# A graph network on one core: 36 sorted blocks instead of 32, 21 gathered instead of 20, and the gather lists made ahead of the first panel

## The chip, the cores and the metric

The kernel runs on one core of one Trainium2 chip. The metric is the device time of one execution in microseconds (us). The engines are named as in the profile: PE (matmuls; PEld its weight loads), DVE (vector), ACT (scalar), POOL (GpSimd, which here mostly issues DMAs with an index for each row), SP (issues plain DMAs).

## What is computed

6250 nodes with 256 features, 100000 random edges, sorted by destination. Cut to what matters:

```python
def agg(h):
    return jax.ops.segment_sum(h[src], dst, num_segments=N)
for l in range(NL - 1):                       # three layers, 256 wide
    h = x + agg(x)
    h = relu(h @ W1s[l] + b1s[l])
    h = relu(h @ W2s[l] + b2s[l])
    x = h @ W3s[l] + b3s[l]
h = x + agg(x)                                # the last layer, 64 wide inside
h = relu(h @ cW1 + cb1)
h = relu(h @ cW2 + cb2)
return h @ cW3 + cb3
# ahead of it: h = max(layernorm(x), 0) goes in; behind it: x + result
```

All of it is float32. The graph is drawn at run time, so the kernel has to look at the edges itself.

## The kernel before

The nodes stand in 49 tiles of 128 (`NT`). Since a sum over edges and a product commute, the table from which each layer reads holds z = h @ W1 already (W3 of a layer is multiplied into W1 of the next), and a layer is: sum z over the edges, add the own row and the bias, relu, two products, store the next z.

**Two ways to sum over the edges.** A block is 128 destination nodes.

- *Multiplied* blocks: an adjacency matrix (counts, one byte each) of 6250 sources by 128 destinations is built in layer 0 and kept in DRAM (`mat`). A *panel* is 3 or 4 such blocks side by side, 384 or 512 columns. `product(l, p)` (L2060 on) walks over the 49 source tiles in the order `ORDER`; for each, ACT casts the bytes to float (`a`, L2052), and PE does four matmuls (agg, L2087: two column halves, and z split into a high and a low part in `XY`). Behind a panel come its relu (L2098) and the MLP (`ps`, L1567 and L1666, with `zz` on DVE, L1671), spread between the matmuls of the next panel.
- *Gathered* blocks: for these POOL fetches, for each k, the k-th neighbour's row of all 128 nodes at once, with one indirect DMA (L1761). DVE adds the rows up two at a time (`sums`, L1798), adds the own row (`u`, L1812 and L1816), PE transposes the block (`pt`, L1825), and it joins the MLP. A block costs as many gathers as its largest degree.

To make gathering cheap the nodes of 32 blocks (`NS`) are *ranked by degree* ("s" blocks; block 0 has the smallest degrees); the other 17 blocks ("u") stay as they are. Of the s blocks the 20 lowest are gathered in layers 0 to 2 (284 rows of each node in all, and in layer 0 one more for each block, the own row), 19 in the last layer (267). The other 29 (30 in the last) are multiplied. Layers 0 to 2 take eight panels, the last layer too.

**Results.** z of u blocks goes back to its place in `XY` and to the table directly. s blocks hold nodes from anywhere, so POOL *scatters* them, one indirect DMA for each block (`place_rows`, L600, with a one-word memset as a mark between two, L598). Once all are placed, `pairs_back` reads the s tiles back two at a time (`turned`, three in flight) and splits them into `XY` (ACT L1391, DVE L1392). `ORDER` walks over the u tiles first, to give this time. The first gather of the next layer waits for all writes to the table. In the last layer s blocks are added into the output, in the same way.

**The rush.** The last gathered block of layers 0 to 2 is a single one. It has its own short MLP (`rush`, L1498, L1514, L1527), since the scatter behind it opens the next layer.

**What sets the order.** The program is written out whole by a planner in Python. It keeps a clock of the PE work it has emitted (`passed`), and class `ByNode` spreads the gathers over a layer: `begin` sets the first date (the clock plus a lag of 9 or 12 us) and a pace from the layer's PE work, less `close`; `ready` says when the sums of a pair of rows are emitted on DVE; `send` emits the gathers, each tied behind the last paced PE instruction (`after`), so POOL cannot run ahead of PE by more than the plan. Constants: `AHEAD_OF` (how much ahead of the layer's end the gathering shall be done), `SLOW` (us planned for a unit ahead of the first panel). Every engine works strictly in its written order.

**Layer 0.** Ahead of the panels, input rows are normalized, and the edges are looked up and the nodes ranked (until about 125 us). Then `build` makes the adjacency in *units*: DVE compares (hi and lo one-hots, L1234), PE multiplies them (bp, L1288), ACT casts (`at`, L1296), SP stores. `PRE` = 28 units come ahead of the first panel, the others between the matmuls of the panels. The *lists* (`listed`, L1848 on) say which node stands at each rank and where its edges are. For every four s blocks DVE makes three tiles (`lane`, `block` and `moved`, L1854 to L1863), PE sums them (L1870), then POOL fetches the edge lists (L1886), and DVE makes row indices of them (`idxN`). Four values, as bf16 digits in `V` = 6 columns, are carried to the ranks: the node (two digits), its degree, and the start of its edges (three digits). In before all this stands in the first panel, a step at every other source tile; later it makes the codes of the s blocks that are multiplied (12 of them, with one that is built in any case).

Of the kernel before, what the change touches and what calls it, by code (L numbers as in the profile page):

```python
# [9 lines left out]
F32 = mybir.dt.float32  # L10
# [9 lines left out]
P = 128  # L20
# [400 lines left out]
def sorted_edges(  # L421
# [69 lines left out]
    NS = 32  # L491
# [3 lines left out]
    seq = [("u", b) for b in range(NS, NT - 3)] + [("s", b) for b in range(NS - 1, NS - 13, -1)] + [  # L495
        ("u", b) for b in range(NT - 3, NT)] + [("s", NS - 13)]
    early = [(0, 3)] + [(b, 4) for b in range(3, 23, 4)] + [(23, 3), (26, 3)]
    wide = [(b, 4) for b in range(0, 20, 4)] + [(20, 3), (23, 3), (26, 3)]
# [3 lines left out]
    nodes_of = [[(16, 4), (12, 4), (8, 4), (4, 4), (1, 3), (0, 1)]] * NLAYER + [  # L502
        [(15, 4), (11, 4), (7, 4), (3, 4), (1, 2), (0, 1)]]
# [35 lines left out]
    V = 6  # L539
    what = const.tile([P, NS, V], BF16, name="what")  # L540
# [354 lines left out]
    def ranking(pool):  # L895
# [5 lines left out]
        nc.gpsimd.tensor_copy(what[:, :, 0], place[:, 0:1].to_broadcast([P, NS]))  # L901
        nc.gpsimd.tensor_copy(what[:, :, 1], colf[:, :NS])
# [46 lines left out]
        nc.scalar.copy(what[:, :, 2], ps[:, :NS])  # L949
# [14 lines left out]
        at = pool.tile([P, NS], I32, name="at_i", bufs=1)  # L964
        nc.vector.tensor_tensor(at, ps[:, :NS], begins, OP.add)
# [36 lines left out]
        bits = pool.tile([P, 3, NS], I32, name="bits", bufs=1)  # L1002
        nc.vector.tensor_scalar(bits[:, 0], at, P - 1, None, op0=OP.bitwise_and)
        nc.vector.tensor_scalar(bits[:, 1], at, 7, None, op0=OP.arith_shift_right)
        nc.vector.tensor_scalar(bits[:, 2], at, 14, None, op0=OP.arith_shift_right)
        nc.vector.tensor_scalar(bits[:, 1], bits[:, 1], P - 1, None, op0=OP.bitwise_and)
        nc.vector.tensor_copy(what[:, :, 3:], bits.rearrange("p v g -> p g v"))
# [119 lines left out]
    with tc.manual_schedule():  # L1127
# [261 lines left out]
        def split(j, m, z):  # L1389

            nc.scalar.copy(XY[:, j:j + m, :C], z[:, :m, :])  # L1391
            later(1, lambda: nc.vector.tensor_tensor(XY[:, j:j + m, C:], z[:, :m, :],  # L1392
                                                     XY[:, j:j + m, :C].bitcast(F32), OP.subtract))
# [7 lines left out]
        def bring():  # L1401
            while wanted and lent[0] < BACK:
# [11 lines left out]
                def back(j=j, z=z):  # L1414
                    split(j, 1, z)
                    later(1, given)
# [7 lines left out]
        def pairs_back(l):  # L1424
# [6 lines left out]
            def more_pairs(wait):  # L1431
                while left and out[0] < PAIRS:
# [6 lines left out]
                    def back(j=j, z=z):  # L1439
                        split(j, 2, z)  # L1440
                        later(1, done)
# [7 lines left out]
            more_pairs(6)  # L1449
# [12 lines left out]
        def store(l, runs, m):  # L1462

            key = f"table{l + 1}"
            for rows, k, kind, b in runs:
# [17 lines left out]
                if kind == "u" and all((l, j) in used for j in fresh):  # L1483
                    split(b, k, rows)
# [223 lines left out]
        class ByNode:  # L1708
# [110 lines left out]
            def finish(self, b, n, g, u):  # L1819
                def turn():  # L1820
# [15 lines left out]
                    if g == n - 1:  # L1836
                        mlp(self.l, [("s", b + q) for q in range(n)], h1, b == 0 or closing, far)

                closing = self.l < NLAYER and b == self.blocks[-2][0]
                far = FAR - 2 if b == self.blocks[-2][0] else FAR  # L1840
                if b == 0 and self.l < NLAYER:
                    halves(2, lambda: rush(self.l, b, u))
                elif b == 0 or closing and g == n - 1:
                    later(2 if b == 0 else 1, turn)
# [4 lines left out]
        def listed(pool, ps_b):  # L1849

            pieces, G4 = [], 4
            for g0 in range(0, NS, G4):
                lane = pool.tile([P, G4, P], BF16, name="lane", bufs=2)
# [8 lines left out]
                moved = pool.tile(shape, BF16, name="moved", bufs=2)  # L1862
# [13 lines left out]
            begin = pool.tile([P, NS], F32, name="begin")  # L1876
            nc.vector.scalar_tensor_tensor(begin, got[:, 4], float(P), got[:, 3], op0=OP.mult,
# [20 lines left out]
            for _ in range(7):  # L1898
                yield
# [322 lines left out]
```

## Time and profile before

| | |
|---|---|
| runs (us) | 1987.24, 1989.18, 1993.07; median 1989.18 |
| the profiled execution (us) | 1992.96, span 1991.1 |
| mean granted clock of PE | 0.966 |
| instructions in the span | 29317 |
| first agg matmul | 153.31 us |
| layer 0 ends (last panel's relu) | 672.88 us |
| layer 1, layer 2 end | 1112.49, 1550.53 us |

The span is what the trace covers; 1.9 us of the execution lie around it. Lines such as L2087 are lines of the kernel. In a group "x66 | 62.7, 949 | 20.1 <-PE agg L2087 10.1" means 66 instructions, 62.7 us busy, 949 ns each, 20.1 us of idle time in front of them, of which 10.1 ended with that release. In a window's row the columns are the stretch, its length, then busy us of PE, PEld, DVE, ACT and POOL with instruction counts, the granted clock of PE as a share, the share of the DMA engines and GB/s. In the timeline the columns are start, duration, engine, line and operation, and in brackets the idle time in front and what ended it.

### The profile page before, as it was taken

The numbers are of one execution on the slowest core, as the hardware profiler recorded it, in microseconds if no ns is written. First come the engines' busy times: TensorE is split into PE (matmuls) and PEld (weight loads), VectorE is DVE, ScalarE is ACT, GpSimd is POOL, SyncE is SP. The second block draws the span as 40 slices with busy tenths as digits, with TensorE's granted clock in tenths as the row PEclk, the third lists the DMA queues.
The fourth block names the chain that finished last, engine by engine and source line by source line (L and its number), as shares of the span: only waits on it lengthen the run. The fifth ranks groups of instructions, "written<-read, shape, count | busy, mean of one in ns | idle before, by whom it ended". The sixth has DMA issues, their size and how long they took to land. (4 is left out here: it accounts for less than half of the span.)

```text
span 1991.1 us, 29317 instructions
## 1 busy us (share of the span) xinstructions
PE 1853.7 (93%) x9334; PEld 1483.0 (74%) x9334; DVE 915.1 (46%) x1915; ACT 1210.6 (61%) x2370; POOL 1338.7 (67%) x1496
## 2 busy tenths in 40 slices
PE   4868999999999899999999899999999899999896
PEld 3746666776788777777898777777898777777774
DVE  6789788676564243332333343333334353332232
ACT  3766666676666476566566376565665576665562
POOL 2521777777777566676777566677777567777775
PEclk9878999999999999999999899999999999999898
DMA  5523665666556485565566575555566676665663
GB/s 176 176 97 115 182 195 168 203 215 217 168 174 211 157 281 181 154 199 172 178 189 212 166 232 164 163 174 165 165 195 197 193 223 208 173 180 149 147 181 81
DMA packets 247119, 357.22 MB, mean 179 GB/s; under 512 B 33368, under 2 KB 201880, under 8 KB 246666
## 3 DMA queue, kind: packets, MB, share of 16 engines
q0 software_dynamic: 65584, 167.88, 29.2%
q1 hardware_dynamic: 179184, 184.72, 28.6%
q10 hardware_dynamic: 2186, 2.65, 0.4%
q8 instruction: 75, 1.23, 0.2%
q14 instruction: 90, 0.74, 0.1%
HBM read 289.20 MB, written 70.92 MB: 181 GB/s over the span
## 5 line engine op out<-in xcount | busy, mean ns | idle before, releaser
L2087 PE MATMUL agg<-a,XY 128*128 128x512 f32 (+1 forms) x6272 | 1471.4, 387 | 14.5 <-ACT a L2052 11.0
L1761 POOL DMA_INDIRECT rows<-table,idxN x1119 | 1076.6, 962 | 422.0 <-PE agg L2087 207.1
L2087 PEld LDWEIGHTS agg<-a,XY 128*128 128x128 f32 x6272 | 1150.1, 191 | 212.5 <-ACT a L2052 21.2
L2052 ACT CAST a<-at 128x512 fp32r<-128x512 uint8 (+1 forms) x1561 | 876.7, 585 | 328.6 <-PE agg L2087 317.9
L1798 DVE TENSOR_TENSOR sums<-sums,rows 128x512 f32<-128x512 f32 x471 | 328.5, 697 | 650.2 <-DMA rows<-table,idxN 627.0
L1296 ACT CAST at<-bp 128x392 uint16<-128x392 f32 x213 | 102.8, 488 | 119.9 <-PE bp L1288 115.8
L1567 PE MATMUL ps<-h,w 128*128 128x512 f32 (+1 forms) x312 | 132.5, 568 | 4.1 <-DVE zz L1671 3.1
L600 POOL DMA_INDIRECT table<-zz,ids x96 | 96.5, 1005 | 55.8 <-DVE zz L1533 23.0
L1666 PE MATMUL ps<-w,h 128*128 128x256 f32 x576 | 133.2, 384 | 0.0
L1666 PEld LDWEIGHTS ps<-w,h 128*128 128x128 f32 x576 | 110.8, 194 | 15.1
L1288 PE MATMUL bp<-hi,lo 128*128 128x98 bf16 x964 | 88.6, 219 | 32.5 <-DVE lo L1234 25.2
L1288 PEld LDWEIGHTS <-lo 128*128 128x128 bf16 x964 | 54.3, 103 | 86.1 <-DVE lo L1234 42.4
L1234 DVE TENSOR_TENSOR lo<-lanes,pairs 128x512 bf16<-128x512 bf16 x240 | 99.3, 423 | 31.4 <-PE bp L1288 30.1
L1567 PEld LDWEIGHTS ps<-h,w 128*128 128x128 f32 x312 | 60.0, 194 | 56.7 <-issue 38.4
L1671 DVE TENSOR_TENSOR zz<-ps,w 128x512 f32<-128x512 f32 x78 | 49.6, 647 | 103.2 <-PE ps L1666 102.1
L1570 ACT ACTIVATE h<-ps,bias 128x512 f32<-128x512 f32 (+1 forms) x78 | 49.8, 656 | 55.8 <-PE ps L1567 55.8
L1833 ACT ACTIVATE h<-pt,bias 128x256 f32<-128x256 f32 (+1 forms) x80 | 32.7, 460 | 83.3 <-PE pt L1825 83.3
L1234 DVE TENSOR_TENSOR hi<-hi,pairs 128x784 bf16<-128x784 bf16 x120 | 69.3, 578 | 4.2
L1234 DVE TENSOR_TENSOR hi<-cols,pairs 128x784 bf16<-128x784 bf16 x120 | 67.2, 560 | 0.6 <-ACT pairs L1222 0.6
L1886 POOL DMA_INDIRECT lane<-padded,at x20 | 20.3, 1016 | 65.5 <-PE bp L1288 59.7
L1392 DVE TENSOR_TENSOR XY<-turned,XY 128x512 fp32r<-128x512 f32 x48 | 32.7, 694 | 67.4 <-ACT XY L1391 67.3
L600 POOL DMA_INDIRECT out_dram<-zz,ids x32 | 50.8, 1588 | 15.2 <-issue 7.1
(261 smaller groups left out, 958.5 us busy)
## 6 DMA issues: line engine op xcount, KB each, us to landing
at<-mat SPq DMA_DIRECT2D x112, 448.0 KB
mat<-at SPq DMA_DIRECT2D x30, 784.0 KB
at<-mat SPq DMA_DIRECT2D x62, 336.0 KB
rows<-table,idxN POOLq DMA_INDIRECT x1119
turned<-table SPq DMA_DIRECT2D x48, 256.0 KB
at<-mat SPq DMA_DIRECT2D x50, 224.0 KB
at<-mat SPq DMA_DIRECT2D x84, 112.0 KB
own<-zz SPq DMA_DIRECT2D x59, 128.0 KB
```

Of the source, the lines that this page charges most:

```text
L600: got = nc.gpsimd.indirect_dma_start(out=ap, out_offset=bass.IndirectOffsetOnAxis(ap=ids[:, b:b + 1], axis=0), in_=sb, in_offset=None, **kw)
L1234: nc.vector.tensor_tensor(o, values, which[:, :, None, :].to_broadcast(shape), op)
L1288: mm = nc.tensor.matmul(bp[:, m * HW:(m + 1) * HW], lo[:, m, :], hi[:, m, :], start=(i == 0), stop=(i == len(sets) - 1))
L1296: nc.scalar.copy(o, v)
L1567: mm = nc.tensor.matmul(ps[:, :w], weights[l][0][:, c, i * P:(i + 1) * P], h1[:, c, :w], start=(c == 0), stop=(c == KC - 1))
L1570: later(soon, lambda: nc.scalar.activation(h2[0][:, i, :w], ps[:, :w], AF.Relu, bias=b2[l][:, i:i + 1]))
L1666: mm = nc.tensor.matmul(o, h2[0][:, c, nodes], w3[:, c, :], start=(c == 0), stop=(c == KC - 1))
L1671: later(soon, lambda: nc.vector.tensor_tensor(z[:, :m, :], v, w3[:, KC:, :].to_broadcast([P, m, C]), OP.add))
L1761: got = nc.gpsimd.indirect_dma_start(out=t[:, c % 2, :], out_offset=None, in_=tables[self.l][:, :], in_offset=bass.IndirectOffsetOnAxis(ap ...
L1798: nc.vector.tensor_tensor(sums, sums, rows.rearrange("p h c -> p (h c)"), OP.add)
L2052: nc.scalar.copy(o, v)
L2087: mm = nc.tensor.matmul(agg[c][:, :w], XY[:, j, o:o + P], a[:, :w], start=(i == 0 and half == 0), stop=(i == NT - 1 and half == 1))
```

## The change

- `NS` goes from 32 to 36; 13 blocks stay unsorted. Layers 0 to 2 gather 21 blocks (291 rows for each node, in layer 0 with own rows 312), the last layer 19 (257 rows). 28 blocks are multiplied in layers 0 to 2: in layer 0 four panels of 3 and four of 4, in layers 1 and 2 seven panels of 4. The last layer keeps its 30 in eight panels. There are 36 scatters a layer and 18 pairs to read back.
- The block that is gathered last, alone, is the one with most rows (block 20 with 17; in the last layer block 18 with 16) and no longer block 0 with 10.
- The lists are made in the stretch ahead of the first panel, one step at each of the 28 units, with three float32 values (node, degree, start of edges) and no digits; the tiles for them are borrowed from the gathers' pool (`rows`). The edge lists of the first two groups of blocks are fetched there, the others in the first panels, between the codes of the s blocks that are multiplied (one step at every third source tile). Gathering in layer 0 begins as soon as the first list is there.
- Planner: `AHEAD_OF` 4 to 8, `SLOW` 1.0 to 1.8; two pairs fewer of delay in front of the first read-back (6 to 4); at the end of every layer all sums are emitted, in before only in the last; the last layer's copies of x into the output (`own_rows`) are spaced otherwise. `renewed` is a check of the program's order and emits nothing.

The diff's core:

```diff
-    NS = 32
+    NS = 36
-    early = [(0, 3)] + [(b, 4) for b in range(3, 23, 4)] + [(23, 3), (26, 3)]
-    wide = [(b, 4) for b in range(0, 20, 4)] + [(20, 3), (23, 3), (26, 3)]
+    early = [(b, 3) for b in range(0, 12, 3)] + [(b, 4) for b in range(12, 28, 4)]
+    wide = [(b, 4) for b in range(0, 28, 4)]
-    nodes_of = [[(16, 4), (12, 4), (8, 4), (4, 4), (1, 3), (0, 1)]] * NLAYER + [
-        [(15, 4), (11, 4), (7, 4), (3, 4), (1, 2), (0, 1)]]
+    nodes_of = [[(16, 4), (12, 4), (8, 4), (4, 4), (0, 4), (20, 1)]] * NLAYER + [
+        [(14, 4), (10, 4), (6, 4), (2, 4), (0, 2), (18, 1)]]
...
-    V = 6
-    what = const.tile([P, NS, V], BF16, name="what")
+    V = 3
+    what = const.tile([P, NS, V], F32, name="what")
...
-            more_pairs(6)
+            more_pairs(4)
...
-                if self.l == NLAYER and now[0] >= ends[self.l] - 2:
+                if now[0] >= ends[self.l] - (2 if self.l == NLAYER else 0):
                     return True
...
+                final = b == self.blocks[-1][0]
                 closing = self.l < NLAYER and b == self.blocks[-2][0]
-                if b == 0 and self.l < NLAYER:
+                if final and self.l < NLAYER:
                     halves(2, lambda: rush(self.l, b, u))
...
+            def wide_tile(n, m):
+                t = gath.tile([P, 2, C], F32, name="rows").rearrange("p h c -> p (h c)")
+                return t[:, :G4 * n * m].rearrange("p (g v b) -> p g v b", g=G4, v=n)
             for g0 in range(0, NS, G4):
-                lane = pool.tile([P, G4, P], BF16, name="lane", bufs=2)
+                lane = wide_tile(1, P)[:, :, 0]
...
-                moved = pool.tile(shape, BF16, name="moved", bufs=2)
+                moved = wide_tile(V, NS)
...
-            for b0, n in lists_of:
-                for b in range(b0, b0 + n):
-                    fetch(run[:, starts_of[b]:starts_of[b] + wide_of[b]], wide_of[b], b)
-            yield
+            fetch_list(0)
+            yield
+            fetch_list(1)
...
+            for _ in range(3):
+                yield
+            make_list(0)
+            for _ in range(4):
+                yield
+            make_list(1)
...
-        LAGS, CLOSE, AHEAD_OF, NEAREST, CLOSING = (9.0, 12.0), 2.0, 4.0, 5.0, 40.0
+        LAGS, CLOSE, AHEAD_OF, NEAREST, CLOSING = (9.0, 12.0), 2.0, 8.0, 5.0, 40.0
-        COLS, FULL32, TURN, BUILD, SLOW, BURST = 0.457e-3, 1.68e-3, 0.4, 0.25, 1.0, 0.3
+        COLS, FULL32, TURN, BUILD, SLOW, BURST = 0.457e-3, 1.68e-3, 0.4, 0.25, 1.8, 0.3
...
-                if beside is not None and (p or i % 2):
+                if beside is not None and i % 3 == 0:
                     next(lists, None)
...
                 tick(layers[0])
                 layers[0].advance()
+                next(lists)
```

More of the change, by code (lines that the diff above doesn't have):

```diff
@@ L963, in ranking @@
         nc.tensor.matmul(ps[:, :NS], one_b, small, start=False, stop=True)
[L964 to L965 removed]
+        nc.vector.tensor_tensor(what[:, :, 2], ps[:, :NS], begins, OP.add)
         yield
@@ L1950, in listed @@
                     yield
+                if j % 3 == 0:
+                    fetch_list(2 + j // 3)
+                    if j and 1 + j // 3 < len(lists):
+                        make_list(1 + j // 3)
                 if j < HELD:
```

87 lines of the change are left out of this document (44 added, 43 removed).

## The prediction

> **What bounds the kernel now.** I read first the busy shares of the page and its two costliest groups: the line of all engines, then the matmuls that sum over sources (agg) and the row gathers.
>
> ```profile
> PE 1853.7 (93%) x9334; PEld 1483.0 (74%) x9334; DVE 915.1 (46%) x1915; ACT 1210.6 (61%) x2370; POOL 1338.7 (67%) x1496
> L2087 PE MATMUL agg<-a,XY 128*128 128x512 f32 (+1 forms) x6272 | 1471.4, 387 | 14.5 <-ACT a L2052 11.0
> L1761 POOL DMA_INDIRECT rows<-table,idxN x1119 | 1076.6, 962 | 422.0 <-PE agg L2087 207.1
> ```
>
> PE looks like the only bound. An average over stages can hide others, so next came the windows by stage: PE, PEld, DVE, ACT, POOL busy, then the granted clock.
>
> ```profile
> 124.00:153.00 29.00, 12.29 (x112) 8.31 (x112) 27.89 (x66) 14.81 (x40) 3.68 (x3) 0.53 0.35 127
> 153.00:212.00 59.00, 51.84 (x384) 43.20 (x384) 55.15 (x132) 39.48 (x97) 19.12 (x19) 0.94 0.40 122
> 212.00:673.00 461.00, 441.44 (x2609) 332.50 (x2608) 303.94 (x738) 298.94 (x626) 344.00 (x366) 0.98 0.61 192
> 673.00:1112.00 439.00, 427.39 (x1915) 351.65 (x1914) 149.12 (x249) 267.38 (x495) 304.38 (x338) 0.99 0.60 191
> 1112.00:1550.00 438.00, 428.44 (x1918) 353.85 (x1917) 149.69 (x248) 263.71 (x489) 303.36 (x340) 0.98 0.59 181
> ```
>
> The stretch in front of the first panel (124 to 153) belongs to DVE: 27.89 of 29 us. In the first panel (153 to 212) DVE and PE are both nearly full. In the rest of layer 0 and in layers 1 and 2 PE sets the pace, with POOL at about 70%. Two narrower views of POOL, 1403 to 1500 and then 1133 to 1230, say what that 70% means.
>
> ```profile
> L1761 POOL DMA_INDIRECT rows<-table,idxN x66 | 62.7, 949 | 20.1 <-PE agg L2087 10.1 <-issue 5.8 <-PE ps L1567 0.9
> L600 POOL DMA_INDIRECT table<-zz,ids x11 | 10.9, 990 | 2.6 <-issue 2.1 <-DVE sums L1794 0.3 <-DVE sums L1798 0.2
> L598 POOL MEMSET mark<- 1x4 f32 x8 | 0.7, 91 | 0.0
> L1761 POOL DMA_INDIRECT rows<-table,idxN x66 | 62.8, 951 | 36.3 <-PE agg L2087 27.3 <-DVE sums L1798 2.6 <-issue 2.1
> ```
>
> Late in a layer, busy and idle time make up the whole window: 62.7 + 20.1 + 10.9 + 2.6 + 0.7 = 97.0 of 97 us. There the engine is full: a gather costs (62.7 + 20.1)/66 = 1.254 us, a scatter with its mark (10.9 + 2.6 + 0.7)/11 = 1.29. Early in a layer a gather takes 1.50 us, because rows are released only as PE advances. The last view is the timeline at the ends of layers 0 to 2, where the last gathered block is rushed through PE (pt), and its scatter opens the next layer's gathers.
>
> ```profile
> 672.88 1.05 ACT L2098 ACTIVATE h<-agg,bias 128x384 f32<-128x384 f32 x2 [4.74 <-PE agg L2087]
> 680.75 0.44 PE L1498 MATMUL pt<-ident,u 128*128 128x128 f32 x2 [3.45 <-DVE u L1816]
> 1112.49 1.05 ACT L2098 ACTIVATE h<-agg,bias 128x384 f32<-128x384 f32 x2 [0.39 <-PE agg L2087]
> 1119.71 0.69 PE L1498 MATMUL pt<-ident,u 128*128 128x128 f32 x2 [2.79 <-DVE u L1812]
> 1229.46 1.27 ACT L2098 ACTIVATE h<-agg,bias 128x512 f32<-128x512 f32 x2 [0.73 <-PE agg L2087]
> 1550.53 1.05 ACT L2098 ACTIVATE h<-agg,bias 128x384 f32<-128x384 f32 x2 [0.39 <-PE agg L2087]
> 1551.93 0.95 POOL L1761 DMA_INDIRECT rows<-table,idxN  x1 [0.30 <-issue]
> 1557.88 0.44 PE L1498 MATMUL pt<-ident,u 128*128 128x128 f32 x2 [2.93 <-DVE u L1812]
> ```
>
> The ACTIVATE rows mark panel ends. PE already waits about 3 us per layer for the rushed block, so POOL is nearly as long as PE. From rush to rush a middle layer takes 1119.71 − 680.75 = 438.96 and 1557.88 − 1119.71 = 438.17 us. I make the sum between these points.
>
> **The change, part by part.** Where numbers are of the changed program's order, they are counts of instructions.
>
> *Lists in front of the first panel.* On DVE, in that stretch, before: compares alone (hi, lo) that build the adjacency.
>
> ```order
> L1234 TENSOR_TENSOR hi<-cols,pairs 128x784
> L1234 TENSOR_TENSOR hi<-hi,pairs 128x784
> L1234 TENSOR_TENSOR lo<-lanes,pairs 128x512
> L1303 TENSOR_TENSOR at<-at,ident 128x128
> L1234 TENSOR_TENSOR lo<-lanes,pairs 128x512
> ```
>
> And after (the tiles called rows hold lane and moved, the one-hots that sort the nodes):
>
> ```order
> L1227 TENSOR_TENSOR hi<-cols,pairs 128x784
> L1227 TENSOR_TENSOR hi<-hi,pairs 128x784
> L1859 TENSOR_TENSOR rows<-lanes,goal 128x512
> L1863 TENSOR_TENSOR block<-lanes,goal 128x144
> L1868 TENSOR_TENSOR rows<-block,what 128x432
> L1227 TENSOR_TENSOR lo<-lanes,pairs 128x512 x2
> ```
>
> Nine such groups of three moved onto the full engine. Their prices are in the first panel's groups of before (DVE, then PE; the page's row of sums stands last):
>
> ```profile
> L1234 DVE TENSOR_TENSOR lo<-lanes,pairs 128x512 bf16<-128x512 bf16 x40 | 16.1, 418 | 1.4 <-PE bp L1288 1.4
> L1234 DVE TENSOR_TENSOR hi<-hi,pairs 128x784 bf16<-128x784 bf16 x20 | 11.3, 567 | 0.7
> L1234 DVE TENSOR_TENSOR hi<-cols,pairs 128x784 bf16<-128x784 bf16 x20 | 11.2, 558 | 0.0
> L1863 DVE TENSOR_TENSOR moved<-block,what 128x768 bf16<-128x768 bf16 x8 | 7.7, 958 | 0.3
> L1854 DVE TENSOR_TENSOR lane<-lanes,goal 128x512 bf16<-128x512 bf16 x8 | 5.5, 683 | 0.0
> L1858 DVE TENSOR_TENSOR block<-lanes,goal 128x128 bf16<-128x128 bf16 x8 | 2.3, 282 | 0.0
> L1880 DVE SCALAR_TENSOR_TENSOR at<-got,begin 128x32 int32<-128x32 f32 x1 | 0.2, 192 | 0.0
> L1870 PE MATMUL sums<-moved,lane 128*128 128x192 bf16 x32 | 4.4, 263 | 1.0 <-DVE moved L1863 1.0
> L1288 PE MATMUL bp<-hi,lo 128*128 128x98 bf16 x156 | 14.3, 215 | 5.9 <-DVE lo L1234 5.9
> L1798 DVE TENSOR_TENSOR sums<-sums,rows 128x512 f32<-128x512 f32 x471 | 328.5, 697 | 650.2 <-DMA rows<-table,idxN 627.0
> L1886 POOL DMA_INDIRECT lane<-padded,at x20 | 20.3, 1016 | 65.5 <-PE bp L1288 59.7
> ```
>
> A group costs 0.683 + 0.29 + 0.958 × 432/768 = 1.51 us; nine cost 13.6. About 24 short operations (copies, list indices, limits) at some 0.2 each add 5, and three sums at 0.697 add 2: 21 us. DVE is in order and must also wait for what it asked for: a list reads four fetches, 4 × (1.016 + 0.30) = 5.3 us and a landing, with some 3 us of compares between; the first sums wait for rows behind eleven fetches. I take 6, bounded by 0 and 13. So **+27** (21 to 34). Nothing hides it; PE has 12.29 us of work there.
>
> [...]
>
> *The first panel.* It loses list work (7.7 + 5.5 + 2.3 on DVE, 4.4 on PE) and 11 of 39 build units (44 of 156 bp matmuls): on DVE 11 × (16.1 + 11.3 + 11.2)/39 = 10.9. DVE falls from 55.15 to about 44, with 13 sums and the code of two blocks added; PE to 51.84 − 4.4 − 44 × 0.092 = 43. I take 50 us for 59, **−9** (bounds −14 and 0), since waits for rows remain.
>
> *The rest of layer 0.* One block fewer is multiplied. The price of width comes from two views of PE, 1230 to 1343 and 1452 to 1492; the next two rows are of 212 to 673.
>
> ```profile
> L2087 PE MATMUL agg<-a,XY 128*128 128x512 f32 x393 | 95.4, 400 | 0.0
> L2087 PE MATMUL agg<-a,XY 128*128 128x384 f32 x197 | 36.2, 342 | 0.0
> L1288 PE MATMUL bp<-hi,lo 128*128 128x98 bf16 x696 | 62.0, 211 | 10.4 <-DVE lo L1234 7.6 <-ACT at L1296 2.6
> L1825 PE MATMUL pt<-ident,u 128*128 128x128 f32 x38 | 7.5, 281 | 3.3 <-DVE u L1816 3.3
> ```
>
> 95.4/393 = 0.243 and 36.2/197 = 0.184 us, so a block is 196 × 0.059 = 11.5 us. The 11 units come back here: 44 × 62.0/696 = 3.9. The first gather of before, on POOL's timeline, is
>
> ```profile
> 213.81 0.94 POOL L1761 DMA_INDIRECT rows<-table,idxN  x1 [0.30 <-issue]
> ```
>
> Rows are now gathered from the stretch on, so the 3.3 us wait of pt should go. **−11** (−7 to −14). Layer 0 ends 27 − 9 − 11 = 7 us later.
>
> *The rush.* PE at the end of layer 1, before:
>
> ```order
> L1567 MATMUL ps<-h_11943,w_8247 128x384 x4
> L2087 MATMUL agg<-a,XY 128x512 x4
> L1498 MATMUL pt<-ident,u 128x128 x2
> L2087 MATMUL agg<-a,XY 128x512 x4
> L1514 MATMUL ps<-h1s,w_8247 128x128 x4
> ```
>
> And after:
>
> ```order
> L2106 MATMUL agg<-a,XY 128x512 x16
> L1497 MATMUL pt<-ident,u 128x128 x2
> L2106 MATMUL agg<-a,XY 128x512 x4
> L1513 MATMUL ps<-h1s,w_8319 128x128 x4
> L1566 MATMUL ps<-h_11701,w_8319 128x512 x4
> ```
>
> Before, pt stands four matmuls into the next layer, behind the last panel's first product; now four matmuls ahead of the end, in the panel's own last source tile: about 1.7 us before the end, if the rows are there. In layer 0 POOL has room (344 of 461 us), so I take that: 672.88 + 7 − 1.7 = 678.2 against 680.75, **−2.6**.
>
> *Layers 1 and 2.* Gathers go from 284 to 291 and scatters from 32 to 36; PE loses 11.5 us in each. After the second panel the program still has 220 gathers and 30 scatters ahead of the last row: 220 × 1.254 + 30 × 1.29 = 314.6 us. The five panels beside them hold 5 × 196 × 0.243 = 238 us of agg and, by PE's groups of layer 1 below (673 to 1112), 5/7 of 44.8 + 44.3 for the MLP: 302 us.
>
> ```profile
> L1567 PE MATMUL ps<-h,w 128*128 128x512 f32 (+1 forms) x104 | 44.8, 575 | 2.4 <-DVE zz L1671 2.1 <-ACT h L2098 0.3
> L1666 PE MATMUL ps<-w,h 128*128 128x256 f32 x192 | 44.3, 383 | 0.0
> ```
>
> So POOL takes over. From rush to rush: 1.7, two panels at 115 (before 1229.46 − 1112.49 = 117.0, of which some 3 was the rush wait), 314.6, and 6 from the last row to pt (1557.88 − 1551.93): 437.3. That is **−1.7** and **−0.9** (±5 each). The 11.5 us of PE turn into waits at pt. AHEAD_OF and SLOW only move the planner's dates; they change none of these counts.
>
> *The last layer.* Its blocks are multiplied as before. The rush stands before the end rather than 7 us behind it, so the first two panels lie wholly behind it: +3. Gathers fall by 10 (−12.5), four scatters to the output are added, by the row below at (50.8 + 15.2)/32 = 2.06 and a mark, +8; most of it in the covered first panels. I take **+2** (−4 to +6).
>
> ```profile
> L600 POOL DMA_INDIRECT out_dram<-zz,ids x32 | 50.8, 1588 | 15.2 <-issue 7.1 <-DVE zz L1650 7.0 <-DVE sums L1798 0.6
> ```
>
> The sum: −2.6 − 1.7 − 0.9 + 2 = −3.2. The profiled execution took 1992.96 us (span 1991.1 and 1.9 around it), 3.8 over the median 1989.18. So 1989.8 profiled, and a median of **1986.0**.
>
> **The rivals.** *A, PE keeps the bound.* If POOL gets rows earlier than my count releases them (the idle 36.3 us early in a layer being used), each middle layer ends with PE: up to 11 us less each, 1964 in full, about 1975 with half. For it: that idle time is there. Against: its releaser is PE's own progress, and the count has it in.
>
> *B, DVE waits in order at the start: slower.* POOL must send 28 fetches and 42 rows by the end of the first panel: 70 × 1.27 = 89 us from about 158 (two thirds through the stretch, when the lists' sums are done), thus to 247, while the panel would end near 230. The sums stand between the compares on DVE, and PE's builds wait for those. It decides if the sums' rows come later than their place, at about 180 and 230: 4 us more in the stretch and 10 in the panel, 1986 + 14 = 2000. For it: the sums' 627.0 us of idle time ended by gathers. Against: that idle time harmed nothing while DVE had slack.
>
> [...]
>
> That the change fails to do what it says is excluded: the order shows lists, widths and rush moved.
>
> **How the numbers follow.** Forecast 0.53, A 0.21, B 0.21, C 0.05. The terms' bounds, taken together, give 1975 to 1997 for the forecast alone; half of A and B reach to 1971 and 2001, my range. A measurement can tell 0.3%, 6 us: 1983.2 to 1995.1 is "same". Faster: A's 0.20 and 0.15 of the forecast, 0.35. Slower: B's 0.18 and 0.03 of the forecast, 0.21. The rest is 0.44.
>
> **What would show it.** First agg near 180; layer 0's end near 680; POOL's busy and idle time filling whole windows from the third panel on in layers 1 and 2; PE waiting at pt for u by some 8 us or more; 437 from rush to rush. If PE has no wait there and the layers take 426, A holds; a first panel ending near 245, B. Wrong would be above all a first agg before 170, or middle layers that differ by over 6 us from 437.

## The result, and the profile after

The changed kernel took 2003.89 us (median of five runs, 2000.80 to 2007.42) against 1989.18: a ratio of 1.0075, with a 95% interval of [1.0054, 1.0096]. That is slower by less than 1%, but clear of the noise. The forecast was 1986.0 and the range ended at 2001. The profiled execution took 2000.80 us, the lowest of the five, and that of before 1992.96, near the top of its own. So the two traces account for 7.8 of the 14.7 us between the medians; what lies between executions of one kernel, no trace shows.

The page's first line and two of its groups, the gathers and the transpositions of gathered blocks, and behind them the transpositions of before:

```profile
PE 1821.2 (91%) x9056; PEld 1421.7 (71%) x9056; DVE 921.2 (46%) x1928; ACT 1173.1 (59%) x2256; POOL 1375.6 (69%) x1547
L1760 POOL DMA_INDIRECT rows<-table,idxN x1130 | 1087.1, 962 | 417.6 <-PE agg L2106 182.4
L1824 PE MATMUL pt<-ident,u 128*128 128x128 f32 x158 | 32.1, 286 | 47.6 <-DVE u L1811 46.5
```
```profile
L1825 PE MATMUL pt<-ident,u 128*128 128x128 f32 x152 | 30.4, 283 | 20.5 <-DVE u L1812 17.2 <-DVE u L1816 3.3
```

PE has 32.5 us less to do and the kernel is longer all the same: 46.5 us of PE's idle time now end with u, the sum of a gathered block (20.5 before). The windows by stage (the stretch ahead of the first panel, the first panel, the rest of layer 0, layers 1 and 2):

```profile
122.00:176.00 54.00, 25.03 (x188) 20.54 (x188) 47.27 (x124) 18.14 (x46) 22.67 (x22) 0.64 0.29 93
176.00:237.00 61.00, 50.78 (x374) 43.76 (x374) 41.57 (x122) 33.30 (x79) 45.78 (x46) 0.87 0.51 154
237.00:684.00 447.00, 426.39 (x2648) 327.45 (x2647) 302.39 (x716) 294.13 (x633) 321.67 (x347) 0.99 0.61 193
684.00:1126.00 442.00, 418.31 (x1716) 322.20 (x1716) 152.49 (x249) 251.80 (x439) 314.38 (x354) 0.97 0.60 190
1126.00:1562.00 436.00, 413.26 (x1714) 318.93 (x1714) 152.20 (x248) 248.23 (x433) 314.14 (x353) 0.99 0.59 181
```

The first panel takes 61 us with no engine near full: DVE 41.57, PE 50.78, POOL 45.78. Two groups of DVE in that window, and the builds' matmuls on PE:

```profile
L1797 DVE TENSOR_TENSOR sums<-sums,rows 128x512 f32<-128x512 f32 x11 | 7.6, 694 | 10.6 <-DMA rows<-table,idxN 10.6
L1281 PE MATMUL bp<-hi,lo 128*128 128x98 bf16 x112 | 10.9, 224 | 9.7 <-DVE lo L1227 9.7
```

DVE stands 10.6 us at sums whose rows have not landed; the compares (lo) are behind them in its order, and PE waits 9.7 us for those. That is a chain from POOL over DVE to PE, and none of the three is full while it lasts.

The ends of layers 0 to 2 on the timeline, with two long waits for an earlier gathered block:

```profile
682.86 0.66 PE L1497 MATMUL pt<-ident,u 128*128 128x128 f32 x2 [8.23 <-DVE u L1815]
684.41 0.69 ACT L2117 ACTIVATE h<-agg,bias 128x512 f32<-128x512 f32 x1 [0.49 <-PE agg L2106]
1097.75 0.69 PE L1824 MATMUL pt<-ident,u 128*128 128x128 f32 x2 [10.10 <-DVE u L1811]
1124.44 0.69 PE L1497 MATMUL pt<-ident,u 128*128 128x128 f32 x2 [3.72 <-DVE u L1811]
1126.02 0.69 ACT L2117 ACTIVATE h<-agg,bias 128x512 f32<-128x512 f32 x1
1534.21 0.69 PE L1824 MATMUL pt<-ident,u 128*128 128x128 f32 x2 [10.12 <-DVE u L1811]
1560.78 0.58 PE L1497 MATMUL pt<-ident,u 128*128 128x128 f32 x2 [5.10 <-DVE u L1811]
1562.26 0.69 ACT L2117 ACTIVATE h<-agg,bias 128x512 f32<-128x512 f32 x1
```

PE waits at pt in each layer: 8.2 us, 10.1 + 3.7, 10.1 + 5.1. POOL from layer 2's first gather to its last scatter but one (1144.3 to 1557.3), and before in the same part (1133.4 to 1553):

```profile
L1760 POOL DMA_INDIRECT rows<-table,idxN x291 | 276.5, 950 | 105.4 <-PE agg L2106 52.6 <-issue 34.4 <-DVE sums L1797 5.0
L600 POOL DMA_INDIRECT table<-zz,ids x31 | 30.7, 990 | 7.4 <-issue 6.3 <-DVE sums L1797 0.8 <-DVE u L1810 0.2
```
```profile
L1761 POOL DMA_INDIRECT rows<-table,idxN x284 | 269.5, 949 | 116.0 <-PE agg L2087 68.1 <-issue 20.7 <-PE ps L1666 7.0
```

The prediction took it as a sign of a full engine that busy and idle time add up to the whole window. They add up so in any window, so this proves nothing; the gap in front of one gather does. The shortest gap in front of a gather on POOL's timeline is 0.30 us. After, without the 9.38 us in front of the first, it is (105.4 − 9.4)/291 = 0.33 us: POOL sends nearly back to back through the whole layer, with some 9 us of slack (291 × 0.03). Before it was (116.0 − 2.4)/284 = 0.40, some 28 us of slack.

One more thing moved. SP's queue at the end of layer 1 and POOL beside it:

```profile
1136.49 2.80 SPq L567 DMA_DIRECT2D turned<-table  x3
1139.40 0.92 SPq L567 DMA_DIRECT2D table<-zz  x2
1140.37 0.91 SPq L572 DMA_DIRECT2D table<-zz  x2
```
```profile
1134.05 0.98 POOL L600 DMA_INDIRECT table<-zz,ids  x1 [8.12 <-DVE zz L1532]
1144.41 0.98 POOL L1760 DMA_INDIRECT rows<-table,idxN  x1 [9.38 <-PE agg L2106]
```

The rush's scatter goes at 1134.05, but the next layer's first gather only at 1144.41, behind the rows of the last panel's own u blocks, which SP sends at 1139.40. Before, those were out 2 us ahead of the rush's scatter, and the gather followed it after 3.6 us.

### The profile page after: what moved, and what is told of

Its sections match the earlier page's. It is cut to its first block, busy times and chain, and to the rows that moved or that the text cites. A ratio compares the mean times of both kernels' runs of the same rounds, so it can differ in the third digit from the quotient of the medians.

```text
span 1998.8 us, 28467 instructions
## 1 busy us (share of the span) xinstructions
PE 1821.2 (91%) x9056; PEld 1421.7 (71%) x9056; DVE 921.2 (46%) x1928; ACT 1173.1 (59%) x2256; POOL 1375.6 (69%) x1547
## 4 chain that ended last, share of the span: by engine, by line
PE 70%; DMA 10%; DVE 4%; issue 4%; POOL 3%; ACT 1%; SPq 0%; DVEq 0%; POOLq 0%; ACTq 0%
PE agg L2106 55%; PE ps L1665 6%; PE ps L1566 5%; DMA rows<-table,idxN 5%; DMA turned<-table 3%; PE bp L1281 2%; POOL rows L1760 2%; DVE sums L1797 1%; PE pt L1824 1%; DMA rows<-table,ids 1%; POOL table L600 1%; DMA table<-zz,ids 1%; PE ps L1580 1%; PE ps L1623 1%; DVE lo L1227 0%
## 5 line engine op out<-in xcount | busy, mean ns | idle before, releaser
L2106 PE MATMUL agg<-a,XY 128*128 128x512 f32 (+1 forms) x5880 | 1424.0, 395 | 11.0 <-ACT a L2070 5.8
L2106 PEld LDWEIGHTS agg<-a,XY 128*128 128x128 f32 x5880 | 1083.7, 191 | 232.3 <-ACT a L2070 15.4
L2070 ACT CAST a<-at 128x512 fp32r<-128x512 uint8 (+1 forms) x1463 | 839.3, 600 | 311.7 <-PE agg L2106 306.6
L600 POOL DMA_INDIRECT table<-zz,ids x108 | 109.2, 1011 | 60.7 <-DVE zz L1532 32.5
L1566 PEld LDWEIGHTS ps<-h,w 128*128 128x128 f32 x296 | 55.8, 191 | 59.7 <-issue 44.1
L1824 PE MATMUL pt<-ident,u 128*128 128x128 f32 x158 | 32.1, 286 | 47.6 <-DVE u L1811 46.5
L600 POOL DMA_INDIRECT out_dram<-zz,ids x36 | 57.1, 1586 | 16.9 <-DVE zz L1649 7.5
L1824 PEld LDWEIGHTS pt<-ident,u 128*128 128x128 f32 x158 | 21.6, 144 | 63.4 <-DVE u L1811 28.9
```

Of the source, the lines that this page charges most:

```text
L600: got = nc.gpsimd.indirect_dma_start(out=ap, out_offset=bass.IndirectOffsetOnAxis(ap=ids[:, b:b + 1], axis=0), in_=sb, in_offset=None, **kw)
L1566: mm = nc.tensor.matmul(ps[:, :w], weights[l][0][:, c, i * P:(i + 1) * P], h1[:, c, :w], start=(c == 0), stop=(c == KC - 1))
L1824: nc.tensor.transpose(self.pt[:, c, i * P:(i + 1) * P], u[:, c * P:(c + 1) * P], ident)
L2070: nc.scalar.copy(o, v)
L2106: mm = nc.tensor.matmul(agg[c][:, :w], XY[:, j, o:o + P], a[:, :w], start=(i == 0 and half == 0), stop=(i == NT - 1 and half == 1))
```

## The experiments

Two theories. **DVE**: the loss is layer 0's start, where sums stand in DVE's order ahead of their rows and the compares behind them. **POOL**: the layers 0 to 2 end when POOL has sent its rows, which have become too many. In the table "layer 0" is its end; ratios are to the kernel before on the same chip, where its median lay between 1988.9 and 1990.2 us. "Lag" is the planner's lag between a layer's first gathers and their sums, 9 us for layer 0 in both kernels. It moves the place of the sums in DVE's order; in the planner's formulas the dates of the gathers don't depend on it.

| run | edit (to the changed kernel unless said) | median us | ratio [95%] | layer 0 |
|---|---|---|---|---|
| e1 | one row less for each gathered block | 1955.86 | 0.9829 [0.9803, 0.9856] | 669.5 |
| e2 | lag 24 | 1982.55 | 0.9957 [0.9941, 0.9972] | 662.0 |
| e3 | lists beside the first panel | 2007.77 | 1.0091 [1.0061, 1.0121] | 688.9 |
| e4 | 20 gathered | 1980.75 | 0.9958 [0.9943, 0.9972] | 684.6 |
| e5 | 20 gathered, lag 24 | 1979.09 | 0.9959 [0.9939, 0.9980] | 676.6 |
| e6 | lag 24, last panel of 3 | 1997.20 | 1.0038 [1.0015, 1.0060] | 673.0 |
| e7 | before with lag 24 | 1982.41 | 0.9961 [0.9940, 0.9981] | 662.0 |
| e8 | lag 24, block 0 last | 1983.49 | 0.9974 [0.9954, 0.9994] | 666.5 |
| e9 | before, 32 bytes unused | 1996.58 | 1.0044 [1.0023, 1.0065] | 678.4 |
| e10 | 32 bytes unused | 2007.19 | 1.0098 [1.0071, 1.0125] | 688.0 |
| e11 | 20 gathered, 32 bytes | 1990.21 | 1.0009 [0.9995, 1.0022] | 685.0 |
| e12 | before, lag 24, 32 bytes | 1983.06 | 0.9967 [0.9950, 0.9985] | 660.1 |
| e16 | lag 24, 160 bytes | 1978.88 | 0.9942 [0.9924, 0.9961] | 666.0 |
| e17 | 20 gathered, lag 24, 96 bytes | 1987.69 | 0.9991 [0.9978, 1.0004] | 677.8 |
| e18 | lag 40 | 2011.08 | 1.0101 [1.0079, 1.0123] | 691.2 |

e13, e14 and e15 are the kernels of e16, e17 and e18 on a chip on which before took 2206 us and they 2302, 2237 and 2306 (ratios 1.043, 1.014 and 1.045). So there the two with 21 gathered blocks stay 4% behind before in spite of the longer lag; why is open, and what follows holds for the chips with some 1989 us for before.

**e1, fewer rows.** It leaves one neighbour's row of each of the 21 blocks out of the sum in layers 0 to 2.

```diff
-                    k, r = len(self.order), caps[b + i] + (l == 0)
+                    k, r = len(self.order), caps[b + i] + (l == 0) - (l < NLAYER)
```

> The changed kernel with one row fewer for each of the 21 gathered blocks in layers 0 to 2 (one neighbour's row of each block is left out of the sum). POOL theory (each of the layers 0 to 2 ends when POOL has sent its gathers and scatters back to back): 21 x 1.25 = 26 us less POOL work in each layer, so PE's waits at the end (8 us at the rush of layer 0, 14 and 17 us at pt in layers 1 and 2) go nearly whole: about 35 us less, a profiled time near 1965, layers 1 and 2 from end to end near 427. DVE theory (the loss is the first panel, where DVE waits in order for rows; the layers behind are set by PE): under 6 us less, layers 1 and 2 within 4 us of 441 and 436.

Measured: 48 us less. The ends of layers 0 to 2 in its trace:

```profile
669.48 0.69 ACT L2117 ACTIVATE h<-agg,bias 128x512 f32<-128x512 f32 x1 [0.49 <-PE agg L2106]
1095.67 1.41 ACT L2117 ACTIVATE h<-agg,bias 128x512 f32<-128x512 f32 x2
1517.79 0.69 ACT L2117 ACTIVATE h<-agg,bias 128x512 f32<-128x512 f32 x1
```

Layers 1 and 2 take 426.2 and 422.1 us, 15.4 and 14.1 less than after, with the same work on PE. In these layers POOL is the bound, as forecast; the DVE theory alone falls. Layer 0 gains 15 too, so the whole gain is larger than the 35 us that POOL theory expected.

**e2, a lag of 24.** The sums of layer 0 come 15 us later in the plan; not one instruction is added, and the gathers keep their planned dates.

```diff
-        LAGS, CLOSE, AHEAD_OF, NEAREST, CLOSING = (9.0, 12.0), 2.0, 8.0, 5.0, 40.0
+        LAGS, CLOSE, AHEAD_OF, NEAREST, CLOSING = (24.0, 12.0), 2.0, 8.0, 5.0, 40.0
```

> The changed kernel with a lag of 24 instead of 9 us between the first list and the first sums of layer 0, so that DVE meets the sums later in its order. DVE theory: its three waits for rows in the first panel (2.5, 3.4 and 4.6 us) go, the panel takes about 51 instead of 60.6 us and the whole some 8 to 10 us less, about 1991 profiled. POOL theory: the panel may be shorter, but POOL sends the same count, so the rush of layer 0 comes at 683 or later all the same and the wait in front of it grows by what the panel gains: 0 to 6 us slower, 2000 to 2007.

Measured: 21 us less, faster than before as well. DVE's sums in its first panel (174 to 226), and the ends of that panel and of layer 0 with the rush:

```profile
L1797 DVE TENSOR_TENSOR sums<-sums,rows 128x512 f32<-128x512 f32 x10 | 6.9, 692 | 0.0
```
```profile
226.53 1.05 ACT L2117 ACTIVATE h<-agg,bias 128x384 f32<-128x384 f32 x2 [0.74 <-PE agg L2106]
661.05 0.66 PE L1497 MATMUL pt<-ident,u 128*128 128x128 f32 x2 [8.12 <-DVE u L1815]
662.02 1.26 ACT L2117 ACTIVATE h<-agg,bias 128x512 f32<-128x512 f32 x2
```

No wait for rows, the first panel at 52 instead of 60.6 us, layer 0 at 662.0 instead of 684.4. The wait at the rush stayed at 8 us and did not grow, so POOL theory's expectation for layer 0 fell: POOL too ended 22 us sooner (last gather at 656.4 instead of 678.3), because its gathers are tied to PE's progress and PE stood less. Behind layer 0 this execution, the longest of its ten, took 9 us more than the profiled one of the changed kernel (1323.4 against 1314.4 us); the 21 us are between the medians.

**e3, the lists back.** Steps of the lists only in the panels.

```diff
-                next(lists)
...
-                if beside is not None and i % 3 == 0:
+                if beside is not None and (p or i % 2):
```

> The changed kernel with the steps of the lists back beside the first panel (at every other source tile there, at each one later), as in the kernel before; 36 sorted blocks and 21 gathered stay. Both theories: first agg near 153 instead of 176. DVE theory: no sums stand in the first panel, it takes some 62 us with the list work, and the whole is about 12 us less, near 1988. POOL theory: the first list is fetched some 25 us later, POOL's 400 instructions of layer 0 end later by as much, the rush stands near 700 instead of 683, and the whole is about 15 us slower, near 2015.

Measured: 4 us slower than the changed kernel by the medians, with intervals that overlap; layer 0 at 688.9. First agg at 153.0, the first panel 51.9 us, but the second 75.5 with 17 us of PE idle, the rows arriving later. Neither number was met, and the sign is POOL's: the place of the lists moves the wait and does not make it.

**e4, 20 gathered.** Block 20 is multiplied again, and the panels are cut as in the kernel before.

```diff
...
-    early = [(b, 3) for b in range(0, 12, 3)] + [(b, 4) for b in range(12, 28, 4)]
-    wide = [(b, 4) for b in range(0, 28, 4)]
+    early = [(0, 3)] + [(b, 4) for b in range(3, 23, 4)] + [(23, 3), (26, 3)]
+    wide = [(b, 4) for b in range(0, 20, 4)] + [(20, 3), (23, 3), (26, 3)]
...
-    nodes_of = [[(16, 4), (12, 4), (8, 4), (4, 4), (0, 4), (20, 1)]] * NLAYER + [
+    nodes_of = [[(15, 4), (11, 4), (7, 4), (3, 4), (0, 3), (19, 1)]] * NLAYER + [
```

> The changed kernel with 20 instead of 21 blocks gathered in layers 0 to 2 (block 20 is multiplied again: panels of 3, 5 x 4, 3, 3 and of 5 x 4, 3, 3, 3; block 19 is gathered last); 36 sorted blocks and the lists ahead of the first panel stay. POOL theory: 17 rows or 21 us less POOL work in each layer against 11.5 us more of PE, so the layers come under PE again: 430 to 436 from rush to rush with waits of a few us, rush of layer 0 near 683 with no long wait, in all 5 to 12 us less than the changed kernel. DVE theory: three times 11.5 us of PE are added and nothing is gained, 25 to 35 us slower than the changed kernel.

Measured: 23 us less, all behind layer 0 (684.6 against 684.4). A part of it is not the edit's. In its trace agg matmuls of 512 columns start every 227 ns, 232 in the kernels ahead of it. e9 to e12 and e16, e17 were made to tell the two apart.

**e5, both.** 

> 20 blocks gathered in layers 0 to 2 and the lag of 24 us together. If DVE's waits for rows in layer 0 and POOL's count in layers 1 and 2 are two separate losses, their gains add: 20 us in layer 0 (a first panel of 52, PE's waits for lo 6 instead of 12 us) and layers 1 and 2 as in the run with 20 blocks (437 and 431 from rush to rush), near 1962. If both runs gained by the same thing (POOL late in layer 0), the sum is no better than the better one: 1975 to 1983.

Measured: 1979.09, hardly better than either. Layer 0 ends at 676.6: with the panels of e4 the planner puts 40 lo compares into the first panel, not 28, and that panel takes 61.5 us; at the lag of 9 (e4) it took 60.2. So the gains did not add, but not for the reason expected.

**e6, a last panel of three blocks,** with the lag of 24.

```diff
-    early = [(b, 3) for b in range(0, 12, 3)] + [(b, 4) for b in range(12, 28, 4)]
-    wide = [(b, 4) for b in range(0, 28, 4)]
+    early = [(b, 3) for b in range(0, 9, 3)] + [(b, 4) for b in range(9, 25, 4)] + [(25, 3)]
+    wide = [(b, 4) for b in range(0, 16, 4)] + [(b, 3) for b in range(16, 28, 3)]
```

> The changed kernel with the lag of 24 us, 21 blocks gathered, and panels that end with three blocks (3, 3, 3, 4, 4, 4, 4, 3 in layer 0; 4, 4, 4, 4, 3, 3, 3, 3 in layers 1 and 2) where the changed kernel ends with four. Theory of the last panel's rows: the next layer's first gather waits for the u rows of the last panel, written 18 to 21 us after its end with four blocks and 12 with three; POOL is full in layers 1 and 2, so each of them gets 6 to 7 us shorter and the last layer begins earlier as well: 15 to 20 us less than with the lag alone, near 1965, although two layers have a panel more. Rival, the rush sets it (its scatter opens the layer): first gathers stay some 20 us behind the rush and the time within 5 us of 1983.

Measured: 15 us slower than with the lag alone. First gathers stood 19.9, 12.0 and 17.2 us behind the layers' ends; with the lag alone (e2) it was 21.0, 14.0 and 18.5, so each came 1 to 2 us early and not 6 to 7. Layer 0 was 11 us longer, with 13.5 us at the rush. The late rows of the last panel are seen in the trace; that they cost time was not shown.

**e7, before with the lag.** The same edit in the kernel before. 

> The kernel before with the lag of 24 us in layer 0 as its only edit. DVE theory: DVE waits there for rows too (61 us in layer 0 in front of sums, 13.5 us of PE waiting for lo), so a part of it goes: 6 to 10 us less than before, near 1981. POOL theory: with the lists fetched from 187 on POOL sends back to back until 673, a later sum changes nothing at the end: within 3 us of before, 1987 to 1993.

Measured: 7 us less than before, as the DVE theory expected. Layer 0 ends 10.9 us earlier. The wait was there before, as the builds' matmuls of before in layer 0 (153 to 673) show; the change deepened it, from 13.5 to 17.6 us of PE waiting for lo.

```profile
L1288 PE MATMUL bp<-hi,lo 128*128 128x98 bf16 x852 | 76.3, 212 | 16.2 <-DVE lo L1234 13.5 <-ACT at L1296 2.6
```

Set beside e2 this run says most. With the lag of 24 us in both, the kernel before takes 1982.41 us and the changed one 1982.55 (both on one chip): the same, where at the lag of 9 they were 14.7 apart. So the whole loss by the change goes when the sums come later. The 3 us that were forecast as a gain are not there either.

**e8, the block of fewest rows last,** with the lag.

```diff
-    nodes_of = [[(16, 4), (12, 4), (8, 4), (4, 4), (0, 4), (20, 1)]] * NLAYER + [
+    nodes_of = [[(17, 4), (13, 4), (9, 4), (5, 4), (1, 4), (0, 1)]] * NLAYER + [
```

> The changed kernel with the lag of 24 us and block 0 (10 rows) gathered last and alone instead of block 20 (17 rows); 21 blocks are gathered as before. If the order of the blocks matters: the closing group of four ends 7 rows or 9 us later than with block 20 last, its MLP and its four scatters come later, and the rush's scatter stands behind them: up to 9 us slower in each of three layers, 1990 to 2005. If POOL's count alone matters (the same 291 rows and 36 scatters): within 4 us of the run with the lag alone, 1979 to 1987.

Measured: within 1 us of e2 by the medians, and the intervals of the two ratios overlap. Which block is last does not matter here.

**e9 to e12, 32 bytes.** An unused tile among the constants shifts all tiles behind it. In e9 to the kernel before, in e10 to the changed one, in e11 to e4, in e12 to e7:

```diff
+    gap = const.tile([P, 8], F32, name="gap")
+    nc.vector.memset(gap, 0.0)
```

> The kernel before with an unused tile of 32 bytes in each partition among the constants, as its only edit. In the runs with 20 gathered blocks and 36 sorted ones the agg matmuls of 512 columns follow each other every 227 ns, in every other run every 232; in their memory map the tiles of a start 32 bytes past a multiple of 64, in the others on one. Theory of the place: the pad brings 227 ns and, where PE is the bound, 6272 x 5 ns = 31 us less, of which POOL's fullness lets some 10 to 25 through: 1964 to 1980. Rival, the 5 ns have another cause (the chip or the hour): 232 ns and 1986 to 1993.

> The changed kernel with the same pad of 32 bytes. Theory of the place: agg at 227 ns; PE has 29 us less to do, but POOL bounds layers 1 and 2 (waits of PE there grow by 6 us each and the layers stay at 441 and 436 from end to end), so only layer 0 and the last layer gain: 5 to 12 us less than the changed kernel, 1992 to 1999. If PE were the bound in layers 1 and 2: all 29 us, 1975.

> 20 gathered blocks with the lists ahead of the first panel (the lag of 9 us) and the pad, which here brings the tiles of a back to a multiple of 64. Agg at 232 ns. It tells how much of the gain of the 20 blocks (23 us against the changed kernel) was the place: if all of it, the time is that of the changed kernel, 2000 to 2007; if POOL's smaller count gains by itself, 1985 to 1995, with layers 1 and 2 near 438 and 434 from end to end.

> The kernel before with the lag of 24 us in layer 0 and the pad. If the two gains add (7 us by the lag, 10 to 25 by the place): 1955 to 1973, faster than both kernels. If POOL takes back what PE gains: 1973 to 1982.

Measured: e9, e10 and e12 kept 232 ns; the theory as put (32 bytes past a multiple of 64) is wrong. e9 was 8 us slower than before by the medians, and e10 3 us slower than the changed kernel; both stay unexplained. e11 lost the 227 ns (234) and took 1990.21: so 20 blocks gain some 14 us at the lag of 9, which fits POOL's smaller count, and the rest of e4's 23 was the spacing. Since an unused tile alone moved e9 by 8 us, this split is rough.

**e16 and e17, other pads.** By the memory maps the tiles of a behind layer 0 start 160 bytes past a multiple of 256 in e4 and e5, and 0, 32 or 192 past it in the others. e16 brings e2 there (`[P, 40]`), e17 takes e5 away from it (`[P, 24]`).

> The changed kernel with the lag of 24 us and the unused tile of 160 bytes, once more, for a chip on which the kernel before takes about 1989 us. Theory of the place modulo 256: agg at 227 ns, 1972 to 1980. Rival: 232 ns and 1979 to 1987.

> 20 gathered blocks, the lag of 24 us and the unused tile of 96 bytes, once more, for a chip on which the kernel before takes about 1989 us. Theory of the place: agg at 232 ns, 1986 to 1992, no better than 21 blocks with the lag. Rival: 227 ns and 1976 to 1985.

Agg of 512 columns in the middle of layer 2, of e16 and then e17:

```profile
L2108 PE MATMUL agg<-a,XY 128*128 128x512 f32 x390 | 92.1, 394 | 0.0
```
```profile
L2108 PE MATMUL agg<-a,XY 128*128 128x512 f32 x380 | 92.8, 401 | 0.0
```

92.1/390 = 0.236 and 92.8/380 = 0.244 us; from start to start 227 and 232 ns. Both as the theory of the place modulo 256 expected. In time it brought e16 about 4 us against e2, and e17 lost 9 against e5. That POOL takes more of it back with 21 blocks is a guess: these differences are no larger than the 8 us of e9. Among kernels that compute everything e16 has the lowest ratio, though its interval overlaps those of e2, e4, e5 and e7; it is faster than before and after. With the lag in place 20 blocks (e17) are 5 us slower than 21 (e2). That does not clear the 21st block: the profiled e17 loses 15.8 us in layer 0, whose panels are cut otherwise, and behind it takes 1309.1 us, where e2 takes 1323.4 (in an execution 5 us over its median) and the changed kernel 1314.4. So behind layer 0 the 21st block seems to cost still.

**e18, a lag of 40.** 

> The changed kernel with a lag of 40 us in layer 0, once more, for a chip on which the kernel before takes about 1989 us. DVE theory: the remaining waits of DVE for rows (21 us with the lag of 24) go, 3 to 6 us less than with 24: 1976 to 1981. POOL theory: the sums come later and the wait at the rush grows from 8 us: 1983 to 1995.

Measured: 2011.08, slower still. The end of its layer 0:

```profile
661.94 0.69 PE L1824 MATMUL pt<-ident,u 128*128 128x128 f32 x2 [6.65 <-DVE u L1815]
690.20 0.66 PE L1497 MATMUL pt<-ident,u 128*128 128x128 f32 x2 [15.05 <-DVE u L1815]
```

Then POOL's longest wait in the first panel (174.7 to 236), and in that panel DVE's waits for edge lists and PE's for lo:

```profile
205.24 0.98 POOL L1760 DMA_INDIRECT rows<-table,idxN  x1 [15.95 <-ACT sums L1793]
```
```profile
L1908 DVE SCALAR_TENSOR_TENSOR some<-run,spot,some 128x56 f32<-128x56 int32 (+1 forms) x2 | 0.6, 275 | 11.2 <-DMA run<-padded,at 11.2
L1281 PE MATMUL bp<-hi,lo 128*128 128x98 bf16 x112 | 10.8, 223 | 11.3 <-DVE lo L1227 11.3
```

60 of layer 0's 312 gathers are left for its last panel, 51 with the lag of 24 and 41 with 9. Too long a lag moves the wait to the end of the layer; 24 lies between the two losses. The first panel takes 61.2 us there, although no sum waits in it: POOL stands 16 us until ACT has read the first rows for the sums, the later edge lists stand behind that gather in its order, DVE waits 11.2 us for edge lists (4.6 in e2's first panel), and PE 11.3 us for lo. It is the same chain with another link.

## Why the prediction was wrong

The forecast was 1986.0 for the median, 1989.8 for a profiled execution. The median was 18 us more, the profiled execution, 2000.80, 11 us more; the traces can speak of the latter. By the prediction's own steps:

- **Lists in front, +27: right, a little dear.** First agg at 176.39 instead of 153.31, +23.1. The three list operations took 0.684, 0.302 and 0.608 us, 1.59 for a group where 1.51 was forecast. In all DVE's busy time rose by 19.1 us where 21 was forecast, its waits by 5.5 where 6 was, and the stretch began 1.5 us earlier (first compare at 123.31 instead of 124.82).
- **The first panel, −9: the step that failed.** It measured 60.6 against 58.5 us, +2. The prediction summed what DVE (44 us) and PE (43) had to do and took 50, so it left 6 us for waits. DVE had 41.57 us of work and stood 10.6 us in front of sums; PE waited 9.7 us for the compares behind them, and its own work took 50.78 us, not 43, at a granted clock of 0.87. The wait is rival B, at the place and nearly at the size it was given in the panel (10 us). B's other 4 us, in the stretch, did not come: sums waited 0.8 us there. So that the median lies near B's 2000 is in part luck. e2 shows the wait by taking it away: 8.4 us in the panel and 22 at the end of layer 0, 2 of them ahead of the first agg; for the same wait returns in later panels. Over layer 0 PE waits 17.6 us for lo in the changed kernel and 6.2 in e2, as these groups of after (176 to 684) and e2 (174 to 662) have it; besides, PE's work there is 6.2 us shorter in e2 (471.0 against 477.2 us).

```profile
L1281 PE MATMUL bp<-hi,lo 128*128 128x98 bf16 x852 | 76.3, 212 | 18.6 <-DVE lo L1227 17.6 <-ACT a L2070 1.0
```
```profile
L1281 PE MATMUL bp<-hi,lo 128*128 128x98 bf16 x852 | 75.7, 211 | 6.5 <-DVE lo L1227 6.2
```

- **The rest of layer 0, −11: within its bounds, but partly by luck.** It took 447 us against 461, −13.7. The prediction did not have the 8.2 us at the rush. They were paid for by PE's busy time, which fell by 15 us where the prediction's block and units make 7.6; why so much is open.
- **The rush, −2.6: failed with the first panel.** "POOL has room in layer 0" was read from 344 of 461 us; with gathers tied to PE, a late PE makes a late POOL, and the last row was asked for at 678.3. The rush stood at 682.86, +2.1 and not −2.6.
- **Layers 1 and 2 at 437.3: right.** 441.6 and 436.3 from rush to rush, POOL nearly back to back, 14 and 15 us of waits at pt. e1 shows the bound. From the end of the second panel to the last row POOL took 319.6 us in both layers, where the prediction had 314.6 (221 gathers at 1.27 us instead of 220 at 1.254), and from there to pt 4.7 instead of 6. Layer 1 is the longer one by its first panel, 62.6 us against 57.4; PE waits 5.6 us there for casts and for the rush's short MLP, 1.7 in layer 2. Why is open. The first gather is late in both (705.45, 22.6 us behind the rush, and 20.0): the prediction let the rush open the layer, and the last panel's own rows did. But behind the second panel 221 gathers were left in both, so that no cost of this shows.
- **The last layer, +2:** 438.0 against 433.2 from the rush to the span's end, +4.8. Up to the last panel's relu it is +1.9; from there to the end it took 19.7 us instead of 16.7. Its first gather is late in the same way, 19.8 us behind the rush instead of 12.7, but that this costs anything is not shown.

The sum of the misses is 4.7 at the rush of layer 0, 4.3 and −1.0 in layers 1 and 2, 2.8 in the last: 10.8. In the 4.7 the first panel alone misses by 11, and the shorter stretch (4) and the shorter rest of layer 0 (3) take part of that back. Rival A found nothing for it. Rival C, a colder clock, went along with B: the first panel of after has a granted clock of 0.87 with 50.78 us busy, that of e2 0.92 with 46.74 for nearly the same matmuls (374 and 371). PE was busy for 83% of the one panel and 90% of the other. No run sets the clock apart from the waits, so none shows what lowers it, or that C, given a chance of 0.05, costs anything by itself.

Open: why the first panel of layer 1 and the end of the last layer are longer, the part of the 14.7 us that the two traces don't hold, and why e9 was slower than before.

## What to carry to other kernels

An operation that is put into an in-order engine's queue ahead of its data holds up everything behind it (here 10.6 us of DVE at sums in the first panel, and 9.7 us of PE that waited for the compares), so work that consumes a slow transfer belongs at least the transfer's real delay behind its request; one number of the plan was worth 21 us here (e2). Put it much further back and the loss returns from the other side (e18). When a change shifts load from the full engine to a nearly full one, count the second one's gaps per instruction (0.40 in before and 0.33 in after, where the shortest seen is 0.30 us), not its busy share. And before a gain is put down to an edit, look whether the unchanged inner loop still runs at its old pitch (227 ns in e4, 232 in after), since an edit that resizes a constant moves every tile behind it. Last, compare two variants stage by stage: e17 is slower than e2 as a whole, and faster behind layer 0.

## What the runs showed of the hardware that was not expected

The pitch of agg matmuls of 512 columns (z as a high and a low part in XY, the moving tile a written mostly by ACT) went with where a starts in each partition, in the runs made here. Behind layer 0 it was 227 ns at 160 bytes past a multiple of 256 (e4, e5, e16), 232 at 0 and 32 (before, after and the others on these chips), 234 at 192 (e11; all medians). The mean time of one in the middle of layer 2 goes the same way: 395 ns in e4 and 394 in e16, against 400 in before and after, 399 in e10 and 401 in e17. In layer 0 the tiles of a stand elsewhere, in before and after at 192 past a multiple of 256, and there these two ran at a median of 234 ns as well. The mean shows no such difference: from start to start, without gaps of 300 ns and more, it is 232.7 ns there in after and 233.5 behind it. The changed program has 3920 agg matmuls of 512 columns behind layer 0 (20 panels of 196); 5 ns each (232 − 227) would be some 20 us of PE, by my estimate. XY, the other operand, starts at the same place modulo 256 in before, after and the runs e2, e4, e5, e9 to e12, e16 and e17, by their memory maps. Whether the place of a itself does it or that of another tile that shifts with it was not tried.
